# A transformer block on one core: two more roots in PSUM, earlier token loads, and the weight folds of the second attention moved to the start

## The chip, the cores and the metric

The kernel runs on one core of one Trainium2 chip. Its engines are named as the profile names them: PE is TensorE (matrix products; PEld is its loading of weights), DVE is VectorE, ACT is ScalarE, POOL is GpSimd, SP is SyncE, which here only issues transfers (DMA). SBUF is the on-chip memory; PSUM is the memory of eight banks that PE writes its results to. The metric is the device time of one execution in microseconds (us); lower is better. A change is judged by the median of several executions.

## What is computed

The input x has shape (2, 256, 128, 128): 2 batches, 256 times, 128 bands, 128 channels, in fp32. Three residual steps follow each other:

```python
xt = _ln(x, ln_t_w, ln_t_b).transpose(0, 2, 1, 3)
x = x + _mha(xt, t_wi, t_bi, t_wo, t_bo, H_T, cm).transpose(0, 2, 1, 3)
xf = _ln(x, ln_f_w, ln_f_b)
x = x + _mha(xf, f_wi, f_bi, f_wo, f_bo, H_F, bm)
xn = _ln(x, ln_n_w, ln_n_b)
h = jax.nn.gelu(xn @ w1.T + b1, approximate=False)
x = x + (h @ w2.T + b2)
```

`cm` is a causal mask over the 256 times, `bm` lets bands see those at most 16 away, and `h` has 512 hidden channels. `_ln` is a layer norm over the channels, `_mha` an attention with 4 heads of 32 channels: `qkv = x @ wi.T + bi`, scores scaled by 1/sqrt(32) plus the mask, softmax, weighted values, `o @ wo.T + bo`.

## The kernel before

**Tiles and groups.** The work is cut into groups of 128 x 512 values (4 tiles of 128 tokens). The 64 groups of each batch over time come first (class `OverTime`, line 646), then, in runs of eight, groups over bands (`OverBands`, line 761) and groups of the feed-forward part (`FeedForward`, line 825). The result over time goes to a buffer in HBM and is read back. Four groups over time share one block ("quad") of input: each of four loads (`load`, in `groups`, line 974) brings one quarter of the partitions for all four groups, so the first group of a quad needs all four loads.

**A group over time.** VectorE takes mean and variance (`statistics`). The inverse root of the variance comes in one of two ways: on GpSimd with a power (`root`, line 407), or on ScalarE by logarithm and exponential (`root_by_scalar`, line 413) with a refinement by three small VectorE instructions on 128x4 values (`refine`, line 425). `root_by_scalar` leaves its estimate in SBUF; `root_in_bank` (line 421) leaves it in the first columns of PSUM bank `b2`. VectorE normalizes. The first four groups are turned by PE (`turn_by_tensor`); later ones by VectorE in blocks of 32 and by a trip through HBM (`turn`: four stores; `fetch`: one load of `xnT`). PE computes queries, keys and values (`queries_keys`, `values`), ScalarE takes them out of PSUM. Scores of one group and of the next are interleaved (`time_scores`, line 747); ScalarE takes exponentials (`first_weights`, `second_weights`), GpSimd sets masked weights to zero and adds. PE computes the sums and the weighted values (`weigh`), VectorE divides (`divide`), PE multiplies by the output weights (`output`), VectorE adds to the residual (`finish`), and every second group SyncE stores.

**Order.** All five engines run in the program order that `run` (line 1266) writes out; no planner moves instructions on this path. Step n of its loop treats group n and pieces of the groups before and after it. `start` (line 1207) brings the first groups up to this state. `banks` names the eight PSUM banks by role; `hand_banks_on` passes the roles on in every step, and `b2` is always bank 7. Waits between engines are put in from the program's accesses; accesses to one PSUM bank by different engines are kept in order even where their columns differ.

**Transfers.** SyncE issues nearly all of them, in program order, each on one of eight semaphores in turn, and an issue can wait for the transfer eight before it. In the loop, steps 0 to 5 issue two token loads each (line 1362), for groups 8 to 19, later steps one. Step 3 also issues `late_weights` (line 67): two rows of output biases, then w2T.

**Folds.** Layer-norm weights and biases are folded into the projection weights: `fold` scales them, `fold_products` (line 1066) multiplies the biases into two columns, `fold_bias` and `fold_value` take these, `fold_row` (line 1088, ScalarE) spreads the value bias over a row, `fold_output` and `add_row` (lines 1094 and 1098) make of it the row that is added to the residual. For the attention over time this happens in `start` and step 0. For that over bands, `fold_over_bands` (line 1141) does it in steps 16 to 22, in the spare half of bank 7, with the rows of the query biases at the end.

**Squares.** A bound on the scores is tested from squares of the weights: `square_keys` and `square_queries` (lines 1112 and 1120) compute them at the last two steps before the first group over bands becomes current, `take_squares` (line 1127) copies them out. If the test fails, a second path with shifted exponentials runs; with the inputs here it does not.

**Opening.** `warm` (line 1047) gives PE products without use while the first tokens arrive.

The helper `InOrder` records every operation at line 897, so nearly all instructions carry that line in the profile; they are told apart by the names of their tiles.

Of the kernel before, what the change touches and what calls it, by code (L numbers as in the profile page):

```python
# [10 lines left out]
F32 = mybir.dt.float32  # L11
BF16 = mybir.dt.bfloat16
I32 = mybir.dt.int32
AF = mybir.ActivationFunctionType
ALU = mybir.AluOpType
# [4 lines left out]
P = 128  # L20
# [5 lines left out]
NT = 4  # L26
# [6 lines left out]
BANK = 512  # L33
# [9 lines left out]
def load_constants(ctx, tc, x, t_wiT, t_woT, f_wiT, f_woT, w1T, w2T, cols, rows):  # L43
    nc = tc.nc
    B, T, FB, C = x.shape
    k = Consts()
# [20 lines left out]
    def late_weights():  # L67
        rows_in(1, 3)
        k.w2T = const.tile([P, k.NI, C], F32, name="w2T_sb")
        sync.dma_start(k.w2T, w2T.rearrange("(j p) c -> p j c", p=P))  # L70
# [9 lines left out]
    k.rows = const.tile([P, 3, C], F32, name="rows_sb")  # L80
    rows_in(0, 1)
    k.wiT.append(weight(f_wiT, 3 * C, "f_wiT_sb"))
    k.woT.append(weight(f_woT, C, "f_woT_sb"))
    k.load_w1T = lambda: setattr(k, "w1T", weight(w1T, k.NI * P, "w1T_sb"))
    k.late_weights = late_weights
    k.ones = const.tile([P, P], F32, name="ones")
# [284 lines left out]
class Group:  # L371
# [41 lines left out]
    def root_by_scalar(self, to=None):  # L413

        path, n = self.path, self.mv.shape[1]
        ln = path.small.tile([P, n], F32, name=f"lnv{n}")
        path.scalar.activation(ln, self.mv[:, :, 1], AF.Ln, bias=path.eps)
        self.root0 = path.small.tile([P, n], F32, name="root0") if to is None else to
        path.scalar.activation(self.root0, ln, AF.Exp, scale=-0.5)

    def root_in_bank(self):
# [480 lines left out]
class BoundedPath:  # L902
# [144 lines left out]
    def warm(self, banks):  # L1047


        for i in banks:  # L1050
# [4 lines left out]
            )  # L1055

    def fold(self, a, engine):

        k, C = self.k, P
        wf = self.once.tile([P, 3 * C], F32, name=f"wf{a}")  # L1060
        col = k.cols[:, 5 * a : 5 * a + 1]
        engine.tensor_scalar(wf[:, 0:C], k.wiT[a][:, 0:C], col, 1.0 / math.sqrt(D), ALU.mult, ALU.mult)
        engine.tensor_scalar(wf[:, C : 3 * C], k.wiT[a][:, C : 3 * C], col, None, ALU.mult)
        k.wf.append(wf)
# [23 lines left out]
    def fold_row(self, a):  # L1088
        k = self.k
        row = self.once.tile([P, P], F32, name=f"orow{a}")  # L1090
        self.scalar.activation(row, k.ones, AF.Copy, scale=self.bv)
        k.orow.append(row)

    def fold_output(self, a, bank):
        self.op = bank[:, 0:P]
        self.tensor.matmul(self.op, self.k.orow[a], self.k.woT[a], start=True, stop=True)

    def add_row(self, a):
        row = self.k.orow[a]
        self.vector.tensor_tensor(row, self.op, self.k.rows[:, a, :], ALU.add)  # L1100

# [10 lines left out]
    def square_keys(self):  # L1112

        k, C = self.k, P
        self.squares = self.halves(self.ps[self.banks["b1"]])
        for a in range(2):
            wk = k.wf[a][:, C : 2 * C]
            self.tensor.matmul(self.squares[:, 0, a], wk, wk, start=True, stop=True)

    def square_queries(self):  # L1120
        k, C = self.k, P
        for a in range(2):
            wq, gq = k.wf[a][:, 0:C], self.squares[:, 1, a]
            self.tensor.matmul(gq, wq, wq, start=True, stop=False)
            self.tensor.matmul(gq, self.br[:, a], self.br[:, a], start=False, stop=True)

    def take_squares(self):
        self.gs = self.once.tile([P, 2, 2, P], F32, name="gs")
        for u in range(2):
            self.scalar.copy(self.gs[:, u], self.squares[:, u])  # L1130

    def bias_rows(self, bank):
        self.brp = self.halves(bank)[0:1, 1]
        for a in range(2):
            self.tensor.matmul(self.brp[:, a], self.k.bq[a], self.k.ident, start=True, stop=True)

    def take_bias_rows(self):
        self.br = self.once.tile([1, 2, P], F32, name="br")
        self.vector.tensor_copy(self.br, self.brp)

    def fold_over_bands(self, i):

        bank = self.ps[self.banks["b2"]]
        spare = bank[:, BANK // 2 : BANK]
        if i == 0:
            self.fold_products(1, spare)
        if i == 1:
            self.fold_bias(1)
            self.fold_value(1)
        if i == 2:  # L1150
            self.fold_row(1)
        if i == 3:
            self.fold_output(1, spare)
        if i == 4:
            self.add_row(1)
        if i == 5:
            self.bias_rows(bank)
        if i == 6:
            self.take_bias_rows()

# [29 lines left out]
    def fold_hidden(self, bank):  # L1190
        k = self.k
        b1p = self.ps[bank][:, P : P + k.NI]
        for j in range(k.NI):
# [13 lines left out]
    def start(self, groups):  # L1207
# [5 lines left out]
        self.k.load_w1T()  # L1213
        self.warm((0, 1, 5, 2, 3, 6))
        first.statistics()
# [21 lines left out]
        self.fold(1, self.gpsimd)  # L1237
        self.fold_back(1, self.gpsimd)
        third.statistics()
        third.root()  # L1240

        time_scores(None, first)
        second.turn_by_tensor(b["b0"], self.vector)
        Attention.place = dict(qp=b["b3"], kp=b["b1"], vp0=b["b0"], vp1=b["b2"])
        first.first_weights(first.early)
        first.first_weights(first.late)
        fourth.statistics()
        fourth.root()
        first.mask_first()
        second.queries_keys()  # L1250
# [4 lines left out]
        second.take_values()  # L1255
        self.fold_row(0)
        fifth.statistics()
# [8 lines left out]
    def run(self, x, out):  # L1266
# [36 lines left out]
        for n in range(len(groups) + 2):  # L1303
# [21 lines left out]
            if old is not None:  # L1325
                old.second_weights(old.late)
                if n == 0:
                    do(4, "root_by_scalar")
                if n + 2 < TURNED:
                    groups[n + 2].turn_by_tensor(b["b0"], self.vector)  # L1330
                if n == 0:
                    self.fold_output(0, self.ps[b["b3"]])
                    self.fold_hidden(b["b3"])
                    self.add_row(0)
                    do(4, "refine")
                do(n - 2, "output")
                if n == run0[0] - 1:
                    self.square_queries()
            if new is not None:
                new.first_weights(new.early[:1])  # L1340
# [7 lines left out]
            if n == 1:  # L1348
                do(5, "root_by_scalar", "refine")
            if 0 < n < 3 * NT - 5:  # L1350
                do(n + 5, "root_in_bank")
            if n + 2 * NT in fours:
                fours[n + 2 * NT].root_in_bank()
            if turn:
                do(n, "second_half", "second_function")
# [3 lines left out]

            if n == 3:  # L1360
                k.late_weights()
            for i in range(2 * n + 8, 2 * n + 10) if n < 6 else (n + 14,):
                do(i, "load")
# [35 lines left out]
            do_at(n + 1, OverBands, "queries_keys", "take_query", "take_key")  # L1399
            self.fold_over_bands(n - 4 * NT)  # L1400
            if n == run0[0] - 2:
# [14 lines left out]
            do_at(n + 1, OverBands, "values", "take_values")  # L1416
            if n == run0[0] - 1:
                self.take_squares()
            if old is not None or new is not None:
# [70 lines left out]
```

## Time and profile before

| What | Value |
|---|---|
| Median of 3 runs | 2654.55 us (2651.78 to 2654.82) |
| Profiled execution, its own time | 2658.0 us |
| Span of that execution, first to last instruction | 2656.1 us |
| Mean granted TensorE clock | 0.997 |
| Busy share: PE, PEld, DVE, ACT, POOL | 99%, 70%, 81%, 69%, 74% |
| DMA queue of the data | 334.41 MB, 50.1% of 16 engines' span |
| PE busy from 0 to 50 us, from 50 to 100 us | 42.19 us, 47.68 us |
| PE busy from 150 to 200 us, from 900 to 950 us | 48.52 us, 47.95 us |
| PE busy from 300 to 350 us | 50.00 us |

The profile is one execution recorded by the hardware. Busy times of PE count modelled ends of pipelined products, so 50.00 us of 50 means that no gap was seen, not that PE works at its peak. A line of the timeline gives start and duration in us, engine, operation, result and inputs, their shape and count, and in brackets how long the engine had been idle and who released it. "Issue" as a releaser means that the profile shows nothing the engine waited for. Fp32 products are recorded as two passes each.

### The profile page before, as it was taken

What the parts mean: (1) busy time and instruction counts of PE and PEld (TensorE: products, weight loads), DVE (VectorE), ACT (ScalarE), POOL (GpSimd) and SP (SyncE); (2) the same over time, 40 slices, a digit from 0 to 9 for tenths busy, and PEclk for the clock granted to TensorE, in tenths of its full rate; (3) what the DMA queues carried; (4) which work ended last, traced back from release to release, by engine and by line L of the source; (5) the groups of instructions that cost most, each with busy time, mean ns of one, the idle gap of its engine ahead of it and who ended that gap; (6) DMA issues with size and microseconds to landing.
All of it is one profiled execution on the core that took longest, in us unless ns stands there. A gap on an engine that the chain in (4) does not pass through costs nothing.

```text
span 2656.1 us, 156474 instructions
## 1 busy us (share of the span) xinstructions
PE 2631.2 (99%) x68692; PEld 1856.4 (70%) x68692; DVE 2148.6 (81%) x6424; ACT 1840.2 (69%) x3553; POOL 1957.8 (74%) x2307
## 2 busy tenths in 40 slices
PE   8999999999999999999999999999999999999998
PEld 5667766666676666767777776677777766777776
DVE  7888888888888887978879779788797797887974
ACT  6888899989989974665755746647557466475573
POOL 5989999999999986667567666675776666757762
PEclk9999999999999999999999999999999999999999
DMA  5555565556566544455444544554454445544443
GB/s 136 152 144 153 148 154 152 150 152 158 147 152 155 125 121 114 121 127 127 118 121 122 128 115 121 131 130 118 116 125 122 117 118 128 131 114 123 120 104 87
DMA packets 469845, 344.97 MB, mean 130 GB/s; under 512 B 43168, under 2 KB 404512, under 8 KB 469152
## 3 DMA queue, kind: packets, MB, share of 16 engines
q1 hardware_dynamic: 468432, 334.41, 50.1%
q8 instruction: 540, 8.85, 1.5%
q14 instruction: 153, 1.25, 0.2%
q10 hardware_dynamic: 720, 0.46, 0.1%
HBM read 167.98 MB, written 166.72 MB: 126 GB/s over the span
## 4 chain that ended last, share of the span: by engine, by line
PE 97%; DVE 2%; issue 0%; ACT 0%; POOL 0%; DMA 0%; SPq 0%; DVEq 0%; POOLq 0%; ACTq 0%
PE bank L897 97%; DVE xh L897 0%; DVE stats L897 0%; DVE bank L897 0%; DVE u L897 0%; DVE z L897 0%; DVE oT L897 0%; DVE vy L897 0%; DVE ln L897 0%; ACT hT L897 0%; ACT p L897 0%; DMA xnT<-turned 0%; POOL pf L897 0%; DVE rstd L897 0%; DVE mv L897 0%
## 5 line engine op out<-in xcount | busy, mean ns | idle before, releaser
L897 ACT ACTIVATE hT<-bank,b 128x512 f32<-128x512 f32 x512 | 347.3, 687 | 517.1 <-PE bank L897 474.0
L897 POOL TENSOR_SCALAR_AFFINE_SELECT pf<-pf 128x512 f32<-128x512 f32 x768 | 478.4, 637 | 187.1 <-ACT pf L897 160.9
L897 PEld LDWEIGHTS bank<-w2T_sb,hT 128*32 128x32 f32 x16384 | 470.8, 110 | 55.5 <-issue 27.8
L897 PE MATMUL bank<-xnT,wf 128*32 128x512 f32 x4096 | 493.7, 592 | 1.5 <-DVE xnT L897 1.5
L897 PE MATMUL bank<-xnT,w1f 128*32 128x512 f32 x4096 | 492.7, 592 | 0.0
L897 PE MATMUL bank<-w2T_sb,hT 128*32 128x128 f32 x16384 | 488.2, 273 | 2.3 <-issue 1.6
L897 ACT ACTIVATE p<-bank 128x512 f32<-128x512 f32 (+1 forms) x1024 | 430.5, 495 | 69.5 <-PE bank L897 68.5
L897 DVE TENSOR_SCALAR xh<-x,mv,rstd 128x160 f32<-128x160 f32 (+1 forms) x1040 | 404.8, 432 | 60.1 <-POOL rstd L897 49.4
L897 POOL TENSOR_SCALAR_AFFINE_SELECT p<-p 128x1024 f32<-128x1024 f32 (+2 forms) x384 | 364.9, 950 | 75.9 <-ACT p L897 67.6
L897 PEld LDWEIGHTS bank<-wf,xnT 128*32 128x32 f32 x8192 | 244.2, 110 | 148.2 <-issue 100.1
L897 DVE BATCH_NORM_STATS2 stats<-x 128x6 f32<-128x128 f32 x1536 | 329.2, 277 | 4.7 <-DMA x<-in_x 2.9
L897 POOL TENSOR_TENSOR p<-p,p 128x512 f32<-128x512 f32 x256 | 324.3, 1289 | 10.7
L897 POOL TENSOR_SCALAR rstd<-mv 128x4 f32<-128x4 f32 x250 | 57.5, 230 | 363.4 <-DVE mv L897 362.2
L897 PE MATMUL bank<-qT,kT 32*64 32x80 f32 (+4 forms) x16384 | 307.2, 273 | 5.9 <-issue 4.4
L897 PEld LDWEIGHTS bank<-xnT,w1f 128*32 128x32 f32 x4096 | 190.8, 110 | 167.1 <-issue 106.6
L897 PEld LDWEIGHTS bank<-qT,kT 32*64 32x64 f32 x16384 | 263.4, 131 | 58.2 <-ACT kT L897 49.4
L897 DVE TENSOR_TENSOR res<-bank,res 128x512 f32<-128x512 f32 (+1 forms) x259 | 170.7, 659 | 157.4 <-PE bank L897 147.3
L897 ACT ACTIVATE pf<-bank 128x512 f32<-128x512 f32 x512 | 266.3, 602 | 37.7 <-PE bank L897 32.3
L897 PE MATMUL bank<-wn,oT 128*32 128x128 f32 x8192 | 287.4, 275 | 0.9 <-DVE oT L897 0.7
L897 PE MATMUL bank<-wf,xnT 128*32 128x128 f32 x8192 | 279.0, 273 | 4.9 <-DVE rstd L897 3.4
L897 DVE STREAM_TRANSPOSE z<-xh 128x512 f32<-128x512 f32 x380 | 270.4, 712 | 13.7
L897 POOL TENSOR_TENSOR rstd<-rstd,mhalf 128x4 f32<-128x4 f32 x250 | 259.8, 1039 | 20.8
(100 smaller groups left out, 3836.3 us busy)
## 6 DMA issues: line engine op xcount, KB each, us to landing
turned<-z SPq DMA_DIRECT2D x1520, 64.0 KB, 2.7
xnT<-turned SPq DMA_DIRECT2D x380, 256.0 KB, 3.1
x<-res SPq DMA_DIRECT2D x256, 128.0 KB, 2.5
x<-x SPq DMA_DIRECT2D x128, 256.0 KB, 4.0
out<-res SPq DMA_DIRECT2D x252, 128.0 KB, 2.3
x<-in_x SPq DMA_DIRECT2D x124, 256.0 KB, 4.4
x<-in_x SPq DMA_DIRECT2D x4, 128.0 KB, 3.0
x<-in_x SPq DMA_DIRECT2D x6, 64.0 KB, 2.7
```

What stands on the lines that cost most here:

```text
L897: return self.tc.keep_in_program_order(emit(*args, **kwargs))
```

## The change

Parts of the diff, by what they do:

- The fifth and sixth group's root estimates go to the last four columns of bank 7 (`root_in_spare`) instead of SBUF.
- `start` loads groups 8 to 11 as well; steps 0 and 1 load two groups each (12 to 15), step 2 and all later ones one. The second row of output biases is loaded with the first at the opening; the third row comes at step 3 and w2T at step 5.
- `warm` at the opening has four products instead of six.
- The folds for the attention over bands go to `start`: its bias products and 16 small products (`stay_warm`) stand behind the turn of the second group; both bias rows are spread by GpSimd instead of ScalarE; both output rows are computed at step 0 and added in one instruction. `fold_over_bands` is gone. The hidden biases move to the last columns of their bank.
- The rows of the query biases follow the squares of the keys, and ScalarE copies them. The squares of the queries go ahead of the outputs of that step and use two banks; their copies go ahead of the reciprocals of that step.

```diff
@@ -65,7 +65,6 @@
             sync.dma_start(k.rows[:, i, :], rows[i : i + 1, :].partition_broadcast(P).squeeze(1))
 
     def late_weights():
-        rows_in(1, 3)
         k.w2T = const.tile([P, k.NI, C], F32, name="w2T_sb")
         sync.dma_start(k.w2T, w2T.rearrange("(j p) c -> p j c", p=P))
 
@@ -78,11 +77,11 @@
     tokens(2, 2, (sync, sync))
     k.woT = [weight(t_woT, C, "t_woT_sb")]
     k.rows = const.tile([P, 3, C], F32, name="rows_sb")
-    rows_in(0, 1)
+    rows_in(0, 2)
     k.wiT.append(weight(f_wiT, 3 * C, "f_wiT_sb"))
     k.woT.append(weight(f_woT, C, "f_woT_sb"))
     k.load_w1T = lambda: setattr(k, "w1T", weight(w1T, k.NI * P, "w1T_sb"))
-    k.late_weights = late_weights
+    k.late_weights, k.late_rows = late_weights, lambda: rows_in(2, 3)
     k.ones = const.tile([P, P], F32, name="ones")
     nc.vector.memset(k.ones, 1.0)
     k.ident = const.tile([P, P], F32, name="ident")
@@ -418,6 +417,10 @@
         self.root0 = path.small.tile([P, n], F32, name="root0") if to is None else to
         path.scalar.activation(self.root0, ln, AF.Exp, scale=-0.5)
 
+    def root_in_spare(self):
+        path = self.path
+        self.root_by_scalar(path.ps[path.banks["b2"]][:, BANK - self.mv.shape[1] :])
+
     def root_in_bank(self):
         path = self.path
         self.root_by_scalar(path.ps[path.banks["b2"]][:, 0 : self.mv.shape[1]])
@@ -1054,6 +1057,10 @@
                 bank, self.k.ones, self.k.ident.unsqueeze(1).to_broadcast([P, n, P]), start=True, stop=True
             )
 
+    def stay_warm(self, n, column):
+        for i in range(n):
+            product(self, column, self.k.ident, self.k.ones[:, 0:1])
+
     def fold(self, a, engine):
 
         k, C = self.k, P
@@ -1087,17 +1094,19 @@
 
     def fold_row(self, a):
         k = self.k
-        row = self.once.tile([P, P], F32, name=f"orow{a}")
-        self.scalar.activation(row, k.ones, AF.Copy, scale=self.bv)
+        if a == 0:
+            self.orow = self.once.tile([P, 2, P], F32, name="orow")
+        row = self.orow[:, a]
+        self.gpsimd.tensor_scalar(row, k.ones, self.bv, None, ALU.mult)
         k.orow.append(row)
 
-    def fold_output(self, a, bank):
-        self.op = bank[:, 0:P]
-        self.tensor.matmul(self.op, self.k.orow[a], self.k.woT[a], start=True, stop=True)
-
-    def add_row(self, a):
-        row = self.k.orow[a]
-        self.vector.tensor_tensor(row, self.op, self.k.rows[:, a, :], ALU.add)
+    def fold_output(self, bank):
+        self.op = self.halves(bank)[:, 0]
+        for a in range(2):
+            self.tensor.matmul(self.op[:, a], self.k.orow[a], self.k.woT[a], start=True, stop=True)
+
+    def add_rows(self):
+        self.vector.tensor_tensor(self.orow, self.op, self.k.rows[:, 0:2, :], ALU.add)
 
     def fold_back(self, a, engine):
         k = self.k
@@ -1116,47 +1125,26 @@
         for a in range(2):
             wk = k.wf[a][:, C : 2 * C]
             self.tensor.matmul(self.squares[:, 0, a], wk, wk, start=True, stop=True)
+        brp = self.squares[0:1, 1]
+        for a in range(2):
+            self.tensor.matmul(brp[:, a], k.bq[a], k.ident, start=True, stop=True)
+        self.br = self.once.tile([1, 2, P], F32, name="br")
+        self.scalar.copy(self.br, brp)
 
     def square_queries(self):
         k, C = self.k, P
+        self.gq = [self.halves(self.ps[self.banks["a2"]])[:, 1, 0], self.squares[:, 1, 1]]
         for a in range(2):
-            wq, gq = k.wf[a][:, 0:C], self.squares[:, 1, a]
-            self.tensor.matmul(gq, wq, wq, start=True, stop=False)
-            self.tensor.matmul(gq, self.br[:, a], self.br[:, a], start=False, stop=True)
+            wq = k.wf[a][:, 0:C]
+            self.tensor.matmul(self.gq[a], wq, wq, start=True, stop=False)
+        for a in range(2):
+            self.tensor.matmul(self.gq[a], self.br[:, a], self.br[:, a], start=False, stop=True)
 
     def take_squares(self):
         self.gs = self.once.tile([P, 2, 2, P], F32, name="gs")
-        for u in range(2):
-            self.scalar.copy(self.gs[:, u], self.squares[:, u])
-
-    def bias_rows(self, bank):
-        self.brp = self.halves(bank)[0:1, 1]
+        self.scalar.copy(self.gs[:, 0], self.squares[:, 0])
         for a in range(2):
-            self.tensor.matmul(self.brp[:, a], self.k.bq[a], self.k.ident, start=True, stop=True)
-
-    def take_bias_rows(self):
-        self.br = self.once.tile([1, 2, P], F32, name="br")
-        self.vector.tensor_copy(self.br, self.brp)
-
-    def fold_over_bands(self, i):
-
-        bank = self.ps[self.banks["b2"]]
-        spare = bank[:, BANK // 2 : BANK]
-        if i == 0:
-            self.fold_products(1, spare)
-        if i == 1:
-            self.fold_bias(1)
-            self.fold_value(1)
-        if i == 2:
-            self.fold_row(1)
-        if i == 3:
-            self.fold_output(1, spare)
-        if i == 4:
-            self.add_row(1)
-        if i == 5:
-            self.bias_rows(bank)
-        if i == 6:
-            self.take_bias_rows()
+            self.scalar.copy(self.gs[:, 1, a], self.gq[a])
 
     def test(self, a):
 
@@ -1189,7 +1177,7 @@
 
     def fold_hidden(self, bank):
         k = self.k
-        b1p = self.ps[bank][:, P : P + k.NI]
+        b1p = self.ps[bank][:, BANK - k.NI :]
         for j in range(k.NI):
             self.tensor.matmul(
                 b1p[:, j : j + 1], k.w1T[:, j * P : (j + 1) * P], k.cols[:, 11:12], start=True, stop=True
@@ -1211,7 +1199,9 @@
         for group in groups[: 2 * NT]:
             group.load()
         self.k.load_w1T()
-        self.warm((0, 1, 5, 2, 3, 6))
+        for group in groups[2 * NT : 3 * NT]:
+            group.load()
+        self.warm((0, 1, 5, 2))
         first.statistics()
         self.fold(0, self.vector)
         first.root_by_scalar()
@@ -1236,16 +1226,22 @@
         self.fold_back(0, self.gpsimd)
         self.fold(1, self.gpsimd)
         self.fold_back(1, self.gpsimd)
+        self.fold_row(0)
         third.statistics()
         third.root()
 
         time_scores(None, first)
         second.turn_by_tensor(b["b0"], self.vector)
+        self.fold_products(1, self.ps[7])
+        self.stay_warm(4, self.ps[7][:, BANK - 1 :])
+        self.fold_bias(1)
         Attention.place = dict(qp=b["b3"], kp=b["b1"], vp0=b["b0"], vp1=b["b2"])
         first.first_weights(first.early)
         first.first_weights(first.late)
+        self.fold_value(1)
         fourth.statistics()
         fourth.root()
+        self.fold_row(1)
         first.mask_first()
         second.queries_keys()
         second.take_query()
@@ -1253,7 +1249,6 @@
         third.normalize_flat()
         second.values()
         second.take_values()
-        self.fold_row(0)
         fifth.statistics()
         self.hand_banks_on()
 
@@ -1325,17 +1320,17 @@
             if old is not None:
                 old.second_weights(old.late)
                 if n == 0:
-                    do(4, "root_by_scalar")
+                    do(4, "root_in_spare")
                 if n + 2 < TURNED:
                     groups[n + 2].turn_by_tensor(b["b0"], self.vector)
                 if n == 0:
-                    self.fold_output(0, self.ps[b["b3"]])
+                    self.fold_output(self.ps[b["b3"]])
                     self.fold_hidden(b["b3"])
-                    self.add_row(0)
+                    self.add_rows()
                     do(4, "refine")
-                do(n - 2, "output")
                 if n == run0[0] - 1:
                     self.square_queries()
+                do(n - 2, "output")
             if new is not None:
                 new.first_weights(new.early[:1])
             if old is not None:
@@ -1346,11 +1341,13 @@
             if new is not None:
                 new.first_weights(new.early[1:])
             if n == 1:
-                do(5, "root_by_scalar", "refine")
+                do(5, "root_in_spare", "refine")
             if 0 < n < 3 * NT - 5:
                 do(n + 5, "root_in_bank")
             if n + 2 * NT in fours:
                 fours[n + 2 * NT].root_in_bank()
+            if n == run0[0] - 1:
+                self.take_squares()
             if turn:
                 do(n, "second_half", "second_function")
             if n + 3 >= TURNED:
@@ -1358,8 +1355,10 @@
             do_at(n + 2, (OverBands, FeedForward), "fetch")
 
             if n == 3:
+                k.late_rows()
+            if n == 5:
                 k.late_weights()
-            for i in range(2 * n + 8, 2 * n + 10) if n < 6 else (n + 14,):
+            for i in (2 * n + 12, 2 * n + 13) if n < 2 else (n + 14,):
                 do(i, "load")
             do_at(n + 3, (OverBands, FeedForward), "normalize", "turn")
             do_at(n + 4, OverTime, "normalize", "turn")
@@ -1397,7 +1396,6 @@
                     do_at(n + A, OverBands, "statistics", "root")
             do_at(n + 2, OverTime, "queries_keys", "take_query", "take_key")
             do_at(n + 1, OverBands, "queries_keys", "take_query", "take_key")
-            self.fold_over_bands(n - 4 * NT)
             if n == run0[0] - 2:
                 self.square_keys()
             if n in run0[3:5]:
@@ -1414,8 +1412,6 @@
                 do(n - 2, "output", "finish")
             do_at(n + 2, OverTime, "values", "take_values")
             do_at(n + 1, OverBands, "values", "take_values")
-            if n == run0[0] - 1:
-                self.take_squares()
             if old is not None or new is not None:
                 self.hand_banks_on()
 
```

## The prediction

> **What bounds the kernel now.** I read the page first: TensorE (PE) is busy 99% of the span and has 97% of the chain that ended last, so only time in which PE stands still, or runs at a lower clock, can be won:
>
> ```profile
> PE 2631.2 (99%) x68692; PEld 1856.4 (70%) x68692; DVE 2148.6 (81%) x6424; ACT 1840.2 (69%) x3553; POOL 1957.8 (74%) x2307
> ```
>
> Next, PE's waits over the whole span, as "us in total, times, longest":
>
> ```profile
> PE bank L897 <- issue: 6.1, 8, 2.3
> PE bank L897 <- DVE rstd L897: 3.4, 1, 3.4
> PE bank L897 <- POOL ident masks.py:199: 1.5, 1, 1.5
> PE bank L897 <- DVE xnT L897: 1.5, 2, 0.9
> PE bank L897 <- ACT gs L897: 1.0, 1, 1.0
> PE bank L897 <- DVE oT L897: 0.7, 1, 0.7
> PE bank L897 <- ACT bv L897: 0.6, 1, 0.6
> ```
>
> Some 16 us in all, nearly everything in the first 60 us, at 160 to 200 us (band folds) and at 935 to 946 us (squares). The largest, 3.4 us, is followed up on the timeline (start, duration, engine, operation):
>
> ```profile
> 23.70 0.15 DVE L897 SCALAR_TENSOR_TENSOR vy<-mv,root 128x4 f32<-128x4 f32 x1
> 23.89 1.29 DVE L897 SCALAR_TENSOR_TENSOR vy<-vy,root 128x4 f32<-128x4 f32 x1
> 25.21 1.21 DVE L897 SCALAR_TENSOR_TENSOR rstd<-vy,root 128x4 f32<-128x4 f32 x1
> ...
> 36.98 0.16 DVE L897 SCALAR_TENSOR_TENSOR vy<-vy,bank 128x4 f32<-128x4 f32 x1
> ```
>
> ```profile
> 23.87 2.53 POOL L897 TENSOR_TENSOR p<-p,p 128x512 f32<-128x512 f32 x2
> ```
>
> ```profile
> 37.39 0.64 PE L897 MATMUL bank<-wf,xnT 128*32 128x128 f32 x16 [3.43 <-DVE rstd L897]
> ...
> 58.91 2.54 PE L897 MATMUL bank<-qT,kT 32*64 32x128 f32 x52 [2.32 <-issue]
> ```
>
> A refinement on 4 columns takes 0.16 us a piece where the root lies in PSUM, and lasts as long as GpSimd's sum beside it where both inputs lie in SBUF. The fifth and sixth group pay this, so the seventh's refinement, which must leave bank 7 before the fourth group's values go there, ends at 37.3. The 2.32 us at 56.59 have no releaser. In the DMA view one 16 KB instruction packet runs at 56.0 to 56.5, behind stores and loads that fill the queues from 52 to 56 (share 0.95 to 1.05); the 1.21 us at 19.68 look alike (packet at 18.0 to 18.5, backlog until 18.5). PE goes on 2.9 us after the start of either half microsecond. I take both for late instruction blocks.
>
> The table by stretches (width, busy per engine, granted clock, DMA share) has a second price of both long gaps:
>
> ```profile
> 38.00:40.00 2.00, 1.85 (x42) 1.42 (x45) 1.90 (x6) 0.76 (x2) 0.00 (x0) 0.61 0.59 122
> 40.00:42.00 2.00, 2.00 (x50) 1.58 (x39) 1.96 (x10) 0.45 (x2) 0.00 (x0) 0.50 0.40 83
> 42.00:44.00 2.00, 2.00 (x38) 1.44 (x34) 1.22 (x3) 1.81 (x6) 0.96 (x1) 0.50 0.92 265
> 44.00:46.00 2.00, 2.00 (x36) 1.12 (x32) 0.60 (x4) 0.83 (x2) 1.85 (x3) 0.68 0.78 183
> ...
> 60.00:62.00 2.00, 2.00 (x51) 1.84 (x41) 1.93 (x9) 0.94 (x4) 0.00 (x0) 0.50 0.78 192
> ```
>
> The clock is halved after each for one or two stretches of some 3.4 us.
>
> **Part by part: the start, up to the projection of the fifth group (46.36 now).** Two opening 256-column products of 2 passes x 0.43 us go: 1.7 us of PE. The first turn needs xh, ready at 6.6, so at most 1.1 us of this reaches the path, and less if the clock rises later for it: I take 0 (0 to -1.1). In the wait of 0.85 us before the second projection come two bias products (0.5 us, the 128x1 row at 8.80) and 16 small ones (32 passes x 0.03 us, the pace of the 128x32 products): 1.5 us, 0.6 past the cover. They move the instruction block's end forward, so PE meets the stall at 19.68 anyway; with 36 instead of 4 passes left behind it the scores end at 21.6, not 21.2 (+0.4; -1 to +1.5).
>
> Now a wait that the change adds. In the two lists of instructions the root of the fifth group is written to bank 7, and ScalarE's write now waits for PE's last score product there (21.6); the exponential that reads bank 7 waits for VectorE's refinement; and behind that exponential, on ScalarE, stands the one of bank 1, for which PE's next projection waits. So: root 21.9; PE turns the third group until 22.75, folds two outputs (0.2 each) and hidden biases (0.95) until 24.1; VectorE adds biases, 24.2, and both rows (twice the 0.28 us row, less its fixed part: 0.42; 0.3 to 0.56), 24.6; refinement 3 x 0.17 with POOL no longer in the way, 25.1; exponentials 0.38 + 0.53, 26.0. The projection starts at 26.05 instead of 23.25: PE stands still 1.95 us that it doesn't now.
>
> Onward by today's durations: VectorE normalizes and turns the fifth group until 27.5 (now 28.8), and does two groups of statistics until 29.5. PE: projection and values 28.8, scores 30.3, turn 31.3, weights 33.7. ScalarE's exponentials end at 32.1, root of the sixth 32.6; refinement 33.2 (0.6 instead of 3.1); the seventh's root must wait for it (same bank): 33.4; normalize and turn 35.5; seventh's refinement 36.1. PE: projection 35.4, first values 36.0, second values 36.1: the 3.43 us are gone. ScalarE (two reciprocal steps, two exponentials, query, key) ends at 36.9; scores until 38.3; VectorE's division ends at 38.2. Output, sums and weights take 3.1 us at full clock: fifth projection at 41.4 instead of 46.36, **-5.0** (-9 to 0).
>
> **Moved rows of the start.** GpSimd gets two 128x128 products (0.53 to 0.56 us each by its wn rows): ahead of the third root (due at 14.7, used at 16.5) and ahead of the first mask (whose result is used at 28.6): 0. SyncE issues one more row load and four more 256 KB token loads before its first turned store (28.8); 1.1 MB at the 223 GB/s of 10 to 16 us prolong the burst from 18.5 to 23.5. That cover gone, the turned copies would start later; as it is, 0. What it does to the instruction block is the third rival.
>
> **The step at 56 us.** Loads at step 3 fall from two rows, w2T (256 KB) and two token loads to one row and one token load: 1.9 MB to 1.35 MB in some 7 us, w2T two steps later, where one token load is left (1.5 MB, as now at 71 to 76 us, without a stall). Then the block arrives in time. From 56.13 to the next projection PE needs 8.75 us, in the full-clock step before (49.05 to 53.43) 4.38: **-4.37**. The 1.84 us wait of VectorE's statistics at 59 (tokens loaded at 49.8, landing after 8.7) goes too, off the path.
>
> Two rules of the Trainium skill speak against this part. "TensorE: Matmul & The Clock Gate" (HAM oscillation) holds gaps above some 3.4 us to be those that halve the clock. By it the 2.32 us would be worth 2.32, not 4.37. The rows show 0.50 after 2.32 us of gap and 1.00 after 1.21, so I take 4.37, and note that my new gap of 1.95 lies between. "Runtime: NRT & Kernel Launch" (Instruction fetch mechanics) gives PE room for 2048 instructions and calls the fetch mostly hidden; then neither stall could be a fetch (only 222 products and 222 weight loads precede the first) and the 4.37 would stay: 2646. Packet and stall coincide twice, so I keep mine.
>
> **Band folds** leave 160 to 200 us. From the end of the first half of the values to the start of the second, products included: 0.70, 0.48 and 0.60 us (PE timeline): **-1.78**. Their new places are counted above and next.
>
> **Squares.** Bias rows (4 passes, about 0.4 us) fill PE's 0.41 us wait before 935.43: 0. ScalarE's copy of them (402 ns on VectorE) falls into its idle 0.81 us before 936.19: 0, else 0.4. The queries' squares (1.66 us) move ahead of the outputs and cover the 0.66 us wait for oT. The copies of the squares, about 1 us, move into ScalarE's 2.34 us wait before 940.62, so 0.98 us at 945.70 go: **-1.64** (-2.1 to -0.5).
>
> Sum: -5.0 - 4.37 - 1.78 - 1.64 = -12.8. The profiled execution took 2658.0, its span 2656.1: span 2643.3. The median 2654.55 is 3.45 below that execution; the same difference gives **2641.8**.
>
> **Rivals.**
> 1. The late block at 56 us stays or moves to another step (speaks for it: the blocks end 34 products earlier in the step now; against: less traffic): -8.4, 2646.1.
> 2. The PSUM root exchanges one wait for another of the same size in the first 46 us, for instance because the exponentials behind bank 7 delay more than the one projection: -7.8, 2646.8.
> 3. The instruction block at 19.7 us waits behind the whole longer burst: 5 us later, plus about 2.5 us of half clock: -5.3, 2649.3. Against: the block was asked for before the extra loads could be issued, as each waits for the eighth before it.
> 4. Slower: one mechanism, late blocks in the long middle. All block limits move by some 56 instructions; today between 100 and 900 us no PE wait is put down to issue. If the new limit falls where stores of step pairs fill the queues, a stall costs 4.37 each; from the third on (3 x 4.37 = 13.1) the gain is gone, with ten 2686. Against: the whole middle runs at a DMA share of 0.6, not 1.0.
>
> **How the numbers follow.** Chances: forecast 0.60, rivals 0.15, 0.08, 0.12, 0.05. What a measurement can tell from no change is about 0.2%, 5.3 us: below 2649.2 faster. Forecast, first and second rival are faster, and half of the third (the bounds of its start part): 0.89; I say 0.87 faster, 0.08 same, 0.05 slower. Range 2635 to 2650: below, 2.5 us for a shorter start stall and 1.1 for the opening, and some 3 of the start's lower bound; above, the third rival.
>
> **What would show it.** Right: refinements of the fifth and sixth group at 0.5 us; a PE wait of 2 us near 24 us, before the third projection; no PE wait for rstd over 0.5; no 2 us issue wait near 50; clock 1.00 after the start; no PE wait for bv, orow, br or gs; -12 by 950 us and the same after. Wrong: a clock of 0.5 after 24 us, a first block later than 22 us, or issue waits in the middle.

## The result and the profile after

| | Before | After |
|---|---|---|
| Median | 2653.56 us (2650.25 to 2654.82, 12 runs) | 2645.87 us (2642.06 to 2651.24, 12 runs) |
| Profiled execution, span | 2658.0 us, 2656.1 us | 2645.2 us, 2643.3 us |
| Mean granted clock of that execution | 0.997 | 0.998 |

The ratio of the times is 0.9974 [0.9965, 0.9983]: faster by 0.26%, 7.7 us between the medians. The forecast was 2641.8 us with a range of 2635 to 2650: the sign is right, the time lies inside the range, 4.1 us above the forecast. The predicted span, 2643.3 us, is the measured one to the last digit. That is chance: of the four terms of the sum one was seven times too large and two were too small.

PE's waits in the profile after, over the whole span (us in total, times, longest):

```profile
PE bank L900 <- issue: 3.9, 5, 2.4
PE bank L900 <- ACT p L900: 2.1, 1, 2.1
PE bank L900 <- POOL ident masks.py:199: 1.5, 1, 1.5
PE bank L900 <- DVE xh L900: 0.5, 1, 0.5
PE bank L900 <- ACT hT L900: 0.3, 2, 0.2
PE bank L900 <- DVE rstd L900: 0.2, 1, 0.2
PE bank L900 <- DVE u L900: 0.2, 1, 0.2
```

The wait for rstd has fallen from 3.4 to 0.2; those for xnT, gs, oT, bv, br and orow are gone. New is the wait of 2.1 us for p near the start (before's 0.4 us for p was at 935), and the longest issue wait is 2.4 us now. The timeline has both near the start (start, duration, engine, operation, in brackets the idle time before and its releaser):

```profile
17.70 0.92 PE L900 MATMUL bank<-qT,kT 32*64 32x128 f32 x25
21.01 1.97 PE L900 MATMUL bank<-qT,kT 32*64 32x256 f32 x37 [2.39 <-issue]
22.90 1.83 PE L900 MATMUL bank<-ident,xh 128*128 128x128 f32 x8
...
25.01 0.95 PE L900 MATMUL bank<-cols_sb,w1T_sb 128*128 128x1 f32 x8
28.04 3.45 PE L900 MATMUL bank<-xnT,wf 128*32 128x512 f32 x16 [2.07 <-ACT p L900]
...
39.42 0.65 PE L900 MATMUL bank<-wf,xnT 128*32 128x128 f32 x16 [0.21 <-DVE rstd L900]
```

The stall that before had from 19.68 to 20.88 now lasts from 18.62 to 21.01: PE arrives 1.06 us earlier and leaves 0.13 us later. The third projection takes 3.45 us where the fifth takes 1.90. The table by stretches (width; busy time of PE, PEld, DVE, ACT, POOL; granted clock; DMA share; GB/s), cut where the clock changes, says why:

```profile
17.51:20.92 3.41, 1.11 (x39) 0.55 (x28) 2.71 (x11) 1.06 (x4) 1.87 (x3) 1.00 1.08 222
20.92:24.34 3.42, 3.33 (x43) 2.87 (x43) 0.00 (x0) 1.28 (x5) 0.00 (x0) 0.50 0.77 163
24.34:27.75 3.41, 1.62 (x15) 1.54 (x14) 2.26 (x8) 0.89 (x3) 0.18 (x1) 1.00 0.02 5
27.75:31.16 3.41, 3.12 (x16) 0.79 (x20) 3.34 (x16) 1.90 (x4) 3.26 (x4) 0.50 0.18 37
```

After either gap the clock is 0.50 for 3.41 us. VectorE's refinement of the fifth group is as short as forecast, and ScalarE's exponentials start right behind it:

```profile
26.55 0.15 DVE L900 SCALAR_TENSOR_TENSOR vy<-mv,bank 128x4 f32<-128x4 f32 x1
26.73 0.16 DVE L900 SCALAR_TENSOR_TENSOR vy<-vy,bank 128x4 f32<-128x4 f32 x1
26.92 0.16 DVE L900 SCALAR_TENSOR_TENSOR rstd<-vy,bank 128x4 f32<-128x4 f32 x1
...
27.11 1.85 ACT L900 ACTIVATE p<-bank 128x256 f32<-128x256 f32 x4 [2.52 <-DVE rstd L900]
```

At 56 us no wait is left; the projection that before reached at 64.88 comes at 59.79, and the clock is 1.00 from 32 us on:

```profile
56.73 1.08 PE L900 MATMUL bank<-wn,oT 128*32 128x128 f32 x32
...
59.79 1.90 PE L900 MATMUL bank<-xnT,wf 128*32 128x512 f32 x16
```

The two later places, by stretches of 50 us, after and then before:

```profile
150.00:200.00 50.00, 50.00 (x1368) 34.80 (x1364) 42.39 (x126) 45.22 (x104) 46.37 (x43) 1.00 0.59 155
900.00:950.00 50.00, 49.94 (x1370) 34.45 (x1356) 40.03 (x108) 41.25 (x92) 44.48 (x47) 1.00 0.41 101
```

```profile
150.00:200.00 50.00, 48.52 (x1269) 32.58 (x1269) 40.41 (x121) 42.32 (x96) 43.76 (x41) 1.00 0.55 141
900.00:950.00 50.00, 47.95 (x1272) 33.37 (x1268) 38.29 (x112) 40.41 (x91) 44.84 (x44) 1.00 0.41 105
```

To see where the time went I compare the start times of the same PE work (mostly the output product of one group) in both traces. The table gives after minus before, in us:

| Stretch | Forecast | Measured | Stands at |
|---|---|---|---|
| start to the fifth projection (46.36, now 45.63) | -5.0 | -0.7 | -0.7 |
| step at 56 us, to its next projection | -4.37 | -4.36 | -5.1 |
| from there to 80 us | 0 | +0.7 | -4.4 |
| band folds, 140 to 200 us | -1.78 | -3.75 | -8.1 |
| 200 to 930 us | 0 | -0.75 | -8.9 |
| squares, 930 to 950 us | -1.64 | -2.5 | -11.4 |
| to 984 us | 0 | -0.1 | -11.55 |
| 984 us to the end | 0 | -1.25 | -12.8 |

So in the traces the sum is right, but not its parts: the start is nearly missing, and the folds and squares are larger. Between the medians it is 7.7 us, not 12.8. The profiled execution of before took 2658.0 us, 4.4 above the median of its 12 runs; that of after lies 0.7 below its own.

### The profile page after: what moved, and what is told of

It reads as the page before. It is cut to its first block, busy times and chain, and to the rows that moved or that the text cites. A ratio compares the mean times of both kernels' runs of the same rounds, so it can differ in the third digit from the quotient of the medians.

```text
span 2643.3 us, 156538 instructions
## 1 busy us (share of the span) xinstructions
PE 2625.4 (99%) x68720; PEld 1872.0 (71%) x68720; DVE 2143.1 (81%) x6422; ACT 1839.8 (70%) x3553; POOL 1955.0 (74%) x2309
## 3 DMA queue, kind: packets, MB, share of 16 engines
q14 instruction: 153, 1.25, 0.2%
## 4 chain that ended last, share of the span: by engine, by line
PE 99%; DVE 0%; issue 0%; DMA 0%; ACT 0%; ACTq 0%; DVEq 0%
PE bank L900 99%; ACT hT L900 0%; DMA x<-in_x 0%; DMA xnT<-turned 0%; DVE stats L900 0%; DVE res L900 0%; DVE u L900 0%; DVE bank L900 0%; ACT p L900 0%; DVE gs L900 0%; DVE mv L900 0%; DVE z L900 0%; DVE oT L900 0%; DVE xnT L900 0%; DVE vy L900 0%
## 5 line engine op out<-in xcount | busy, mean ns | idle before, releaser
L900 PEld LDWEIGHTS bank<-xnT,w1f 128*32 128x32 f32 x4096 | 206.2, 110 | 153.4 <-issue 94.9
```

Source lines behind the costliest of these rows:

```text
L900: return self.tc.keep_in_program_order(emit(*args, **kwargs))
```

## The experiments

My theory after seeing the traces: at the start only two gaps decide, the longer stall near 19 us (from the loads issued at the opening) and the wait for p (from the root in bank 7, whose reader stands late on VectorE), each with a piece of half clock behind it. The rivals: that the root in PSUM brings nothing against the root in SBUF, and that the earlier loads cost at the start what they bring at 56 us. Each run is after with one thing undone or moved, timed beside before (median there 2653.43 us, 17 runs; after itself was not timed again with them). In the timelines the first line is the end of PE's stall near 20 us.

### The refinement of the fifth group directly behind its root

```diff
-                    do(4, "root_in_spare")
+                    do(4, "root_in_spare", "refine")
...
-                    do(4, "refine")
```

> The changed kernel with one move: the fifth group's refinement stands directly behind its root, ahead of VectorE's copy of the third group's turned values and of the two additions. Theory (the exponential of bank 7 waits for this refinement, and the third projection for the exponential behind it): PE's wait of 2.07 us for ACT p at 28.04 falls below 0.6, ScalarE's wait of 2.52 us for DVE rstd goes, and with a shorter gap the clock keeps more of its rate near 28 us; 2 to 4 us faster than the changed kernel, ratio to the kernel before about 0.996. Rival (the wait at 28.04 only takes up slack that VectorE's later normalizing needs anyway): the wait appears again before 45 us, and the time is that of the changed kernel, ratio 0.997.

Measured: 2643.02 us (2639.79 to 2648.81, 6 runs), ratio 0.9963 [0.9951, 0.9975]; span of the profiled execution 2641.3. PE's timeline:

```profile
20.83 1.08 PE L900 MATMUL bank<-qT,kT 32*64 32x256 f32 x37 [2.12 <-issue]
21.83 1.16 PE L900 MATMUL bank<-ident,xh 128*128 128x128 f32 x8
...
23.28 0.95 PE L900 MATMUL bank<-cols_sb,w1T_sb 128*128 128x1 f32 x8
24.34 1.92 PE L900 MATMUL bank<-xnT,wf 128*32 128x512 f32 x16
```

The wait for p is gone, and so is ScalarE's of 2.52 us for rstd: the third projection follows the hidden biases at once, at 24.34 instead of 28.04. So the wait comes from the reader's place on VectorE, not from the bank as such. The stall is still there, 2.12 us, but this time the clock stays at 1.00 behind it. The fifth projection comes at 40.40, 5.2 us earlier than in after. The median falls by 2.9 us against after; that is within the 2 to 4 us expected, but the intervals overlap, so that this is better than after is likely and not shown.

### The additional token loads behind the first turned stores

```diff
+LATE = {0: range(8, 12), 1: (12, 13), 2: (14, 15), 3: (16,), 4: (17, 18)}
...
-        for group in groups[2 * NT : 3 * NT]:
-            group.load()
...
-            for i in (2 * n + 12, 2 * n + 13) if n < 2 else (n + 14,):
-                do(i, "load")
             do_at(n + 3, (OverBands, FeedForward), "normalize", "turn")
             do_at(n + 4, OverTime, "normalize", "turn")
+            for i in LATE.get(n, (n + 14,)):
+                do(i, "load")
```

> The changed kernel without the six token loads behind w1T at the opening; groups 8 to 11 are loaded in step 0 behind the first turned stores, 12 to 15 in steps 1 and 2, then one a step (two at step 4). Theory (the stall at 18.6 is an instruction block that waits behind the transfers issued before it): the instruction packet runs at 14 to 16.5 us instead of 18.0, the issue wait of 2.39 us falls below 0.8, the clock stays at 1.00 around 20 to 24 us; about 3 to 5 us faster than the changed kernel, ratio 0.9955. Rival (the stall has another cause, or only the loads issued before 11 us count, which are mostly the same): packet at 17.5 to 18.0, wait 2 us or more, ratio 0.997. A second risk: more traffic at 30 to 45 us brings a late block there.

Measured: 2645.57 us (2641.86 to 2648.55, 7 runs), ratio 0.997 [0.996, 0.9981]; span 2643.2. (In every later step too, the load now stands behind that step's turned stores.) PE's timeline, then the stretch after the second gap:

```profile
18.89 1.07 PE L901 MATMUL bank<-qT,kT 32*64 32x256 f32 x37 [0.47 <-issue]
24.36 3.32 PE L901 MATMUL bank<-xnT,wf 128*32 128x512 f32 x16 [2.08 <-ACT p L901]
```

```profile
24.00:26.00 2.00, 1.64 (x8) 0.40 (x12) 1.93 (x6) 1.29 (x3) 1.85 (x3) 0.50 0.00 0
```

The stall shrinks from 2.39 to 0.47 us: the instruction packet begins to run between 16.0 and 16.5 instead of between 18.0 and 18.5 us. In the DMA view of these half microseconds, here and in after, it is the line

```profile
q8 instruction: 1, 0.02, 16.5%
q8 instruction: 1, 0.02, 16.8%
```

The loads at the opening do lengthen the stall. At 56 us no stall comes back, though steps 2 and 4 now issue two loads each. The wait for p stays, with half clock. In the trace the fifth projection is 3.8 us earlier than in after (41.81); the median is 0.3 us lower, which these runs can't tell from nothing: the 3 to 5 us expected did not come.

### The roots of the fifth and sixth group in SBUF again

```diff
-                    do(4, "root_in_spare")
+                    do(4, "root_by_scalar")
...
-                do(5, "root_in_spare", "refine")
+                do(5, "root_by_scalar", "refine")
```

> The changed kernel with the roots of the fifth and sixth group back in SBUF; everything else stays. Theory (a root in PSUM frees the refinement from GpSimd but hangs the exponentials on bank 7): the refinements take about 2.6 us again, the wait of 2.07 us for ACT p at 28.04 goes, a wait for DVE rstd of 2 to 4 us before the fourth group's second values comes back with a half clock after it; 1 to 5 us slower than the changed kernel, ratio 0.998 to 0.9993. Rival (wait for wait, the exchange is worth nothing): within 1 us of the changed kernel, ratio 0.997 to 0.9978.

Measured: 2645.68 us (2642.9 to 2651.6, 6 runs), ratio 0.9968 [0.9956, 0.998]; the profiled execution took 2651.6, its span 2649.7. First PE's timeline, then one of GpSimd and VectorE:

```profile
20.62 1.16 PE L900 MATMUL bank<-qT,kT 32*64 32x256 f32 x37 [2.12 <-issue]
34.60 1.92 PE L900 MATMUL bank<-xnT,wf 128*32 128x512 f32 x16 [1.55 <-DVE xnT L900]
40.72 0.64 PE L900 MATMUL bank<-wf,xnT 128*32 128x128 f32 x16 [3.76 <-DVE rstd L900]
```

```profile
33.04 2.50 POOL L900 TENSOR_TENSOR p<-p,p 128x512 f32<-128x512 f32 x2
...
34.37 1.19 DVE L900 SCALAR_TENSOR_TENSOR vy<-mv,root 128x4 f32<-128x4 f32 x1
35.60 1.21 DVE L900 SCALAR_TENSOR_TENSOR vy<-vy,root 128x4 f32<-128x4 f32 x1
```

The long refinement beside GpSimd's sum is back, and with it the wait for rstd of 3.76 us and one of 1.55 us for xnT; the wait for p is absent. That is the mechanism forecast. Yet the size isn't confirmed, and the 1 to 5 us of loss expected in the median did not come: this execution ran at half clock from 21.5 to 24.9 and from 42.0 to 48.8 us and ended 6.4 us behind after's, while the medians differ by 0.2 us. By the medians the second rival (one wait exchanged for another) is not excluded for this part.

### Loads and w2T as before

```diff
-        for group in groups[2 * NT : 3 * NT]:
-            group.load()
...
-            if n == 5:
                 k.late_weights()
-            for i in (2 * n + 12, 2 * n + 13) if n < 2 else (n + 14,):
+            for i in range(2 * n + 8, 2 * n + 10) if n < 6 else (n + 14,):
```

> The changed kernel with the transfers of the kernel before: groups 8 and 9 at the opening, two loads a step until step 5, w2T at step 3 (the row loads stay where the change put them). Theory (the block at 56 us was late because of step 3's transfers): an issue wait of 1 to 2.5 us comes back between 50 and 60 us with a half clock after it, about 4.4 us slower in that place, and the stall at 18.6 stays as long as in the changed kernel, since its packet was behind the transfers issued before 11 us in both; ratio 0.9985 to 0.9995. Rival (a late block depends on where its limit falls, and the change has moved the limits): no wait at 50 to 60 us, ratio 0.997.

Measured: 2648.23 us (2644.43 to 2650.37, 8 runs), ratio 0.9978 [0.9968, 0.9988]; span 2646.0. PE's timeline, then VectorE's waits from 50 to 66 us, then the stretches with PE's two long gaps:

```profile
19.77 1.07 PE L900 MATMUL bank<-qT,kT 32*64 32x256 f32 x37 [1.02 <-issue]
25.24 1.93 PE L900 MATMUL bank<-xnT,wf 128*32 128x512 f32 x16 [2.07 <-ACT p L900]
...
56.26 0.64 PE L900 MATMUL bank<-p,ones 128*32 128x256 f32 x8 [2.34 <-issue]
...
60.40 1.10 PE L900 MATMUL bank<-wf,xnT 128*32 128x128 f32 x32 [0.48 <-DVE res L900]
```

```profile
DVE stats L900 <- DMA x<-in_x: 4.2, 1, 4.2
```

```profile
26.00:28.00 2.00, 2.00 (x48) 1.07 (x40) 2.00 (x12) 1.63 (x4) 1.92 (x3) 1.00 0.16 33
...
56.00:58.00 2.00, 1.74 (x41) 1.38 (x44) 1.62 (x10) 1.01 (x2) 2.00 (x2) 1.00 0.50 121
```

This run says most. A late block near 56 us is back (its packet begins between 53.0 and 53.5, PE goes on 2.8 to 3.3 us later). By the count of PE's instructions (given below) it is the block after the one that was late in before, so the stall hangs on the traffic of those steps and not on where the blocks end; the changed kernel's blocks alone don't remove it. Behind 2.34 us of gap the clock stayed at 1.00, against the half clock expected, and still the step cost about 4.4 us: from output to output 11.58 us (52.41 to 63.99), where after needs 7.08 and 7.27 in its steps around 56 us. The rest beside the gap I put down to VectorE: it waits 4.2 us for tokens, is late for everything in that step, and PE then waits for the residual (0.48) and for u (0.2); the remaining 1.4 us lie in products that, as I read it, are paced by such inputs, the scores above all (2.65 us from 61.42 to 64.07, where after takes 1.39 and 1.58).

At the start the stall is 1.02 us (expected was one as long as in after), the clock is full throughout although the wait for p is the same 2.07 us (the next part has the reason), and the fifth projection comes at 41.31. The forecast had said 41.4.

### All five together

After minus before by traces at four places, and by medians (us). "Lost to the clock" is half of the time that the trace has at a clock of 0.50 in the first 64 us (10.24 us in before, so 5.1 us).

| Kernel | Fifth projection | 80 us | 984 us | End | Lost to the clock | Medians |
|---|---|---|---|---|---|---|
| after | -0.7 | -4.4 | -11.55 | -12.8 | 3.4 | -7.7 |
| early refinement | -6.0 | -9.6 | -15.8 | -14.8 | 0 | -10.4 |
| late loads | -4.55 | -8.2 | -14.4 | -12.9 | 1.7 | -7.9 |
| roots in SBUF | +3.4 | -0.3 | -7.05 | -6.4 | 5.1 | -7.75 |
| loads as before | -5.05 | -4.4 | -11.3 | -10.1 | 0 | -5.2 |

Two things follow. First, between 80 and 984 us all five gain 6.2 to 7.15 us, whatever the start looks like. All five contain the folds and squares in the same form; neither was run alone, so their part is read from the traces. Second, the traces differ at the start in large part by the clock, and the medians don't follow them. Taking the lost clock out on both sides, before's 5.1 us among it, the end columns become -11.1, -9.7, -9.5, -6.4 and -5.0: the runs with early refinement and with the loads as before now agree with their medians to 0.7 us, late loads and roots in SBUF to 1.6, after itself only to 3.4. From 984 us on nothing differs between the kernels, and their profiled executions still spread from -1.25 to +1.5 us against before's.

That before's profiled execution lost more to the clock than is usual has one more sign. Of 17 executions of before, 7 have a mean granted clock of 0.999, 9 of 0.998 and one of 0.997, the value of the profiled one shown at the start (which is not among the 17). At 0.999 before's median is 2653.1 and after's 2644.4 (7 and 4 executions); at 0.998 it is 2653.7 against 2646.2 (9 and 6). Like with like, the change is worth 7.5 to 8.7 us. Only one execution of each kernel is recorded in full, so that the halvings which other executions lack are the ones at 40 and 60 us is an inference; and the clock is not all, since one execution of before took 2657.98 us at 0.999.

## Why the prediction was right, and where not

**The start (-5.0 forecast, -0.7 in the trace): the step that failed is the stall.** The working said that the products put into the wait before the second projection move the block's end forward, "so PE meets the stall at 19.68 anyway", with 1.2 us of stall and full clock behind it. PE reached it at 18.62 and left it at 21.01, so the 1.06 us won before it were lost in it, and 2.39 us of gap brought half clock. They were won because the opening gave 0.59 us that the sum had at 0 (the second group's turn starts at 12.96 instead of 13.55), and because the products put into the wait fitted it, 1.0 us instead of 1.5, so that the 0.6 us booked past it did not come. The scores ended at 22.98 instead of 21.6. The rest is the second gap: forecast 1.95 us, measured 2.07, and again half clock, for which the sum had nothing. Against the run with the loads as before, where both gaps left the clock alone, the fifth projection is 4.3 us later: 1.24 by the end of the stall (21.01 against 19.77), and 3.1 that fit the 3.4 us lost to the clock.

I had the warning in hand. The working notes half clock after 2.32 us and none after 1.21 us, says that the new gap of 1.95 us "lies between", and then goes on at full clock. The entry that these rows supported was a loss of 0 to 2 us for each gap (4.37 less 2.32 us, what the half clock cost before at 56 us).

**The moved loads (forecast 0 at the start).** The packet began between 18.0 and 18.5 us in before and in after, so it didn't wait for the whole longer burst, and the third rival as it was worded did not happen. But PE needed it 1.06 us earlier. With the loads as before it does come earlier, at 16.5 to 17.0, and with still fewer at 16.0 to 16.5; in the other two kernels with all the loads it runs at 17.5 to 18.0. The loads hold it back, by less than the rival said and more than the forecast's nothing. That it is a block of PE's own program that comes late can be counted: in all six traces the stall falls after 449 of PE's recorded instructions (products, weight loads and those of its sequencer), and the stalls near 56 us after 1729 (before) and 1985 (loads as before). These are 1280 and 1536 more, 5 and 6 times their difference of 256.

**The step at 56 us (-4.37): the size in the trace is right, -4.36, and one cause was missed.** That the block comes in time when the traffic of those steps falls is confirmed by putting the traffic back. The price of 4.37 us was put down to gap plus half clock. The run with the loads as before pays 4.4 us at full clock, because VectorE, whose wait for tokens I had booked as "off the path", becomes the next thing that is late. That fits the medians, 2648.23 against 2645.87: 2.4 us of the same sign, though the intervals overlap.

**The rule on long gaps.** "TensorE: Matmul & The Clock Gate" (HAM oscillation) has gaps above some 3.4 us halve the clock. The gaps of these traces of 1 us and more, from 15 us on, with the clock behind them, are in the next table. Its third column needs a grid that the traces have: in each of the six, all changes in the clock's records lie whole multiples of 3.41 us apart (in after at 20.92, 24.34, 27.75 and 31.16; in the two without a halving the first record and the one at the kernel's end, 771 and 772 intervals later). The first record lies anywhere from 4.42 to 7.72 us. The column gives the largest part of the gap that falls into one interval of the grid:

| Gap, us | Kernel | Largest part in one interval | Clock behind it |
|---|---|---|---|
| 1.02, 1.21, 1.55 | loads as before, before, roots in SBUF | the same | 1.00 |
| 2.07 | after | 1.78 | 0.50 |
| 2.07 | loads as before | 1.07 | 1.00 |
| 2.08 | late loads | 1.52 | 0.50 |
| 2.12 | roots in SBUF | 2.12 | 0.50 |
| 2.12 | early refinement | 1.56 | 1.00 |
| 2.32 | before | 2.32 | 0.50 |
| 2.34 | loads as before | 1.37 | 1.00 |
| 2.39 | after | 2.30 | 0.50 |
| 3.43 | before | 2.36 | 0.50 |
| 3.76 | roots in SBUF | 2.17 | 0.50 |

The rule is too mild here: between 2.07 and 2.34 us the clock was halved four times in seven, and the same 2.07 us before the same product was halved in one kernel and not in another. By the rule alone neither gap of after costs clock, which would have put the fifth projection near the 41.31 of the run with the loads as before; by before's rows alone the gap above 2.32 us costs it. The length of the gap decides neither. The third column does, all but a narrow band: with 1.78 us and more in one interval the clock was halved in the next one or two, six times of six, with 1.37 and less never, and between 1.52 and 1.59 once in four (the earlier 1.59 us of the gap of 3.76 counted in). The 2.07 us of the run with the loads as before lay across two intervals (24.18 is the bound between them), as the rows show beside those of after above:

```profile
20.76:24.18 3.42, 2.41 (x22) 2.31 (x20) 1.52 (x6) 1.53 (x5) 0.00 (x0) 1.00 0.02 5
24.18:27.59 3.41, 2.35 (x40) 1.15 (x44) 3.30 (x14) 2.90 (x6) 2.67 (x3) 1.00 0.01 2
```

Nothing in these runs is seen to set where the grid lies in an execution, so for a gap near 2 us the half clock stays a matter of luck, in the prediction as in the runs. What makes the difference between 1.52 and 1.59 us, and between one halved interval and two, is open.

**Folds (-1.78 forecast, -3.75).** The term was measured at one place per fold, the step in which PE then waits (0.60 for bv, 0.38 for orow, 0.50 for br, each with some 0.1 us around it). It claimed to include the products, but they lie in the step before: 0.61 us at 152, 0.49 at 174.75, 0.60 at 190. After minus before falls twice for every fold: 0.68 and 0.80, 0.56 and 0.59, 0.41 and 0.71. The first of each pair, 1.65 us in all, is the products' own time, the half that I left out of the gain; what the products cost in their new place is part of the start.

**Squares (-1.64 forecast, -2.5).** The three waits at this place, for p 0.41, oT 0.66 and gs 0.98, sum to 2.05 us, and all went. The forecast let the bias rows eat the first of them; PE's busy time from 900 to 950 us rises by 1.99 us. The rest, some 0.45 us, isn't assigned.

**The rivals.** The late block at 56 us is gone and none came up in the middle (PE busy 100.00 of 100 us from 200 to 300, 300 to 400 and 400 to 500 us and at least 99.85 in each hundred up to 900, and its longest issue wait anywhere is the 2.39 us at the start): the first and the slower rival are out, although the measured median lies at the first one's number (2646.1). The second, wait for wait, is true of the first 46 us of this one execution (3.43 us for rstd against 2.07 for p plus clock). In the medians roots in SBUF and roots in PSUM can't be told apart. A kernel with late loads and early refinement together, which by the table should have neither gap, was not tried.

**The median.** The step "the same difference gives 2641.8" took before's profiled execution to lie 3.45 us above its median and after's to lie as far above its own. After's lay 0.7 below. With the span exact, this alone is the 4.1 us of error.

## What to carry to other kernels

Work put into a wait moves PE forward to the next thing it waits for; if that one has a fixed time of its own, as the instruction packet had, the gap grows by what was won. A gap of about 2 us can then cost 1.7 us more for each interval at half clock (3.41 us at 0.50), if, as here, 1.5 us or more of it fall into one interval of the clock's grid. Before a sum is made against one profile, look at the mean clocks of the other executions: if the profiled one has the lowest, its clock losses are not what the change will save in the median. When one engine stalls, check whether another is late in the same step, since it sets the price once the stall is gone.

## What was not expected of the hardware

Equal gaps had unequal consequences, by where they lay on the clock's grid of 3.41 us: 2.07 us before the same product gave a clock of 0.50 with 1.78 us in one interval and of 1.00 with 1.07, and 2.34 us passed without effect. And the end of the stall near 20 us follows the instruction packet in all six traces, 2.7 to 3.1 us after it began to run: from 16.01 to 18.89, 16.77 to 19.77, 17.66 to 20.62, 17.71 to 20.83, 18.03 to 21.01 and 18.13 to 20.88. "Runtime: NRT & Kernel Launch" (Instruction fetch mechanics) calls this fetch mostly hidden; here it is, at 2.1 to 2.4 us, PE's longest wait in after, in early refinement and, near 56 us, in loads as before. Near 20 us the loads queued with the packet take part in setting its size.
